# Fetching part of an embedding lookup row by row from a second DMA queue

## The chip, the cores and the metric

The kernel runs on one core of a Trainium2 chip. The core has a matrix engine (TensorE, PE in the profile), a vector engine (VectorE, DVE), a scalar engine (ScalarE, ACT), a general-purpose engine (GpSimd, POOL) and a synchronisation engine (SyncE, SP). Each engine works through its own instruction list in order and waits on semaphores for the others. Transfers between main memory and the on-chip memory are issued here by GpSimd (gathers, whose row addresses come from an index tile on the chip) and by SyncE (all other transfers). The metric is the time of one execution in device microseconds, lower is better. Before the change it is 5194.64 us, the median of 3 runs (5194.57 to 5196.89).

## The reference

A recommender model scores 16384 examples. Each has 32 token indices into a table of 50000 rows of 300 floats, 3 x 20 indices into small tables of 1000, 5000 and 10000 rows of 64, and 4 single indices into still smaller tables. The token rows and the multi-hot rows are averaged, everything is joined into 748 features, and a wide term adds one scalar per small-table index:

```python
tok = word_emb[token_idx].mean(axis=1)          # 32 rows of 300 each
e1 = emb_mh1[mh1_idx].mean(axis=1)              # e2, e3 alike, 20 rows of 64 each
o1 = emb_oh1[oh1_idx]                           # o2, o3, o4 alike
emb = jnp.concatenate([tok, e1, e2, e3, o1, o2, o3, o4], axis=1)
h = jax.nn.relu(emb @ W1 + b1)                  # 748 -> 1024
h = jax.nn.relu(h @ W2 + b2)                    # -> 512
h = jax.nn.relu(h @ W3 + b3)                    # -> 256
return jax.nn.sigmoid(h @ Wd + bd + wide)
```

## The kernel before

The batch is cut into 128 tiles of 128 examples. Three streams of work run beside each other for different tiles.

**Small tables by counting.** The small tables lie on the chip as `terms` (138 slices of 128 rows, each value split into three bf16 parts). For each example VectorE compares its indices with a ramp (`one_hots`, L344), ScalarE scales one half (L351), TensorE multiplies the two one-hot halves into a count per table row (`counts`, L362), and ScalarE writes the counts out (L365). A tile takes `STEPS` = 11 steps of six examples on each of two halves. In the 11 steps after that, TensorE multiplies the counts with `terms` (`small_sums`, L397, 138 products a tile in four groups that share one PSUM buffer `pg`), and VectorE evicts each group into the feature tile `g` (L387).

**Token rows by gathering.** `tokens()` issues, for each tile, 32 gathers on GpSimd (L279). One gather brings one token column, 128 rows of 1200 bytes, straight from the table. Two gathers fill one buffer of the pool `tok`; VectorE adds them into `tok_sum`, three pairs later in the program (`TOK_LAG`, lines L260 to L267). After the 16th pair the sum goes to `g`.

**Layers.** When a tile has its sums and its token sum, TensorE transposes `g` (L435) into the block `x`, VectorE scales it on the way out (L439). Three tiles form a block (the last two tiles are blocks of one). `mlp` runs the four layers of a block: `layer` (L493) with ScalarE's activations (L504), the last product `po` (L524), the final addition on VectorE (L529), the sigmoid (L530) and the store (L532).

The order is written out by hand in one loop over `n_steps` = 128 x 11 + `WAKE` steps. Everything that a step emits goes into each engine's list in that order. `toks.to(...)` spreads the gathers evenly over all steps; `layers.to(...)` spreads a block's layers from the step in which it becomes ready to the step in which the next one should be (`ready`, L586). `WAKE` = 16 steps come after the last counts, so the counts run ahead of the tokens by up to 16 steps. At `n_steps - EARLY` the first three feature chunks of the last tile are multiplied ahead (`early_part`, L457). If a block becomes ready while another is under way, the other one's remaining layers are emitted at once (L646). SyncE's list holds the index loads (L295, L300), the tables, the weights and the output stores.

Of the kernel before, what the change touches and what calls it, by code (L numbers as in the profile page):

```python
# [8 lines left out]
F32 = mybir.dt.float32  # L9
BF16 = mybir.dt.bfloat16  # L10
FP8 = mybir.dt.float8e3
I32 = mybir.dt.int32
# [6 lines left out]
P = 128  # L19
# [3 lines left out]
D1, D2, D3 = 1024, 512, 256  # L23
TOK_GROUP = 2
TOK_LAG = 3
TOK_BUFS = 7
HOT_BUFS = 3
WAKE = 16
EARLY = 3
BLOCK = 256  # L30
LAYER_TILES = 3
LAST_TILES = 2
# [30 lines left out]
def kernel(  # L63
# [33 lines left out]

    tokp = ctx.enter_context(tc.tile_pool(name="tok", bufs=TOK_BUFS))
    const = ctx.enter_context(tc.tile_pool(name="const", bufs=1))
    idxp = ctx.enter_context(tc.tile_pool(name="idx", bufs=3))  # L100
    keyp = ctx.enter_context(tc.tile_pool(name="keys", bufs=1))
    scp = ctx.enter_context(tc.tile_pool(name="sc", bufs=2))
    ohp = ctx.enter_context(tc.tile_pool(name="onehot", bufs=HOT_BUFS))
    cp = ctx.enter_context(tc.tile_pool(name="counts", bufs=2))
    gp = ctx.enter_context(tc.tile_pool(name="g", bufs=2))
    wp = ctx.enter_context(tc.tile_pool(name="wide", bufs=2))
    xp = ctx.enter_context(tc.tile_pool(name="x", bufs=2))
    hp = ctx.enter_context(tc.tile_pool(name="h", bufs=1))
# [56 lines left out]
    minus_count = const.tile([P, P], BF16, name="minus_count")  # L165
    nc.vector.tensor_single_scalar(minus_count, ident, -1.0 / COUNT, op=ALU.mult)

    def load_tables(part0, tag):
        raw = hp.tile([P, PART, ROW], F32, name="raw", tag=tag)
        for f in SMALL:  # L170
            table, (h0, h1) = tables[f], slices[f]
            full, rest = divmod(table.shape[0], P)
            a, b = max(h0, part0), min(h0 + full, part0 + PART)
            if a < b:
                nc.sync.dma_start(
                    out=raw[:, a - part0 : b - part0, :],
                    in_=table[(a - h0) * P : (b - h0) * P, :].rearrange("(h p) d -> p h d", p=P),
                )
            if rest and part0 <= h0 + full < part0 + PART:
                nc.vector.memset(raw[:, h0 + full - part0, :], 0.0)  # L180
                nc.sync.dma_start(out=raw[0:rest, h0 + full - part0, :], in_=table[full * P :, :])
        return raw

# [71 lines left out]

    def add_up(t, q, rows):

        a, b = rows[:, 0:TOK_D], rows[:, TOK_D : 2 * TOK_D]
        if q == 0:
            nc.vector.tensor_add(tok_sum, a, b)  # L260
        else:
            nc.vector.tensor_add(tok_sum, tok_sum, a)  # L262
            to = tok_sum
            if q == n_groups - 1:
                to = features(t)[:, TOK_AT:G_COLS]
                summed.add(t)
            nc.vector.tensor_add(to, tok_sum, b)  # L267

    def tokens():

        under_way = []
        for n in range(n_all):
            if n < n_all - TOK_LAG:
                t, q = divmod(n, n_groups)
                it = token_indices[t // NSUB][:, t % NSUB, :].bitcast(U32)
                rows = tokp.tile([P, TOK_GROUP * TOK_D], F32, name="tok_rows")
                for r in range(TOK_GROUP):
                    j = q * TOK_GROUP + r
                    nc.gpsimd.indirect_dma_start(  # L279
                        out=rows[:, r * TOK_D : (r + 1) * TOK_D],  # L280
                        out_offset=None,
                        in_=word,
                        in_offset=bass.IndirectOffsetOnAxis(ap=it[:, j : j + 1], axis=0),
                    )
                under_way.append((t, q, rows))
            if n >= TOK_LAG:
                add_up(*under_way.pop(0))
            yield 1

    def load_indices(blk):  # L290

# [121 lines left out]
    class Block:  # L413
# [2 lines left out]

        def __init__(self, first, n):
            self.first, self.n, self.missing = first, n * P, NK * n
            self.x = xp.tile([P, NK, N], F32, name="x")

        def transpose(self, t, ks):

# [34 lines left out]
    def early_part(block):  # L457


        part = []  # L460
        for pair in range(2):
            two = ps_c.tile([P, 2, 512], F32, name="pc")
            for m in range(2):
                part.append(two[:, m, :])
                for k in range(N_EARLY):
                    nc.tensor.matmul(
                        part[-1][:, 0 : block.n],
                        w1_sb[: chunk_k[k], k, (2 * pair + m) * P : (2 * pair + m + 1) * P],
                        block.chunk(k),
                        start=(k == 0),  # L470
                        stop=False,
                    )
        return part

    pending = []

    def flush_outputs():
        while pending:
# [2 lines left out]
    def layer(dst, weights, bias, srcs, n_out, part=None):  # L481


        n = srcs[0].shape[-1]
        for m in range(n_out):
            begun = part is not None and m < 4
            ph = part[m] if begun else ps_h.tile([P, N], F32, name="ph", tag="ph")
            for k, src in enumerate(srcs):
                if begun and k < N_EARLY:
                    continue  # L490
                if k == len(srcs) - 1:
                    flush_outputs()
                nc.tensor.matmul(  # L493
                    ph[:, 0:n],
                    weights[: src.shape[0], k, m * P : (m + 1) * P],
                    src,
                    start=(k == 0),
                    stop=(k == len(srcs) - 1),
                )
                if k < len(srcs) - 1:  # L500
                    yield 1

            def evict(m=m, ph=ph):
                nc.scalar.activation(dst[:, m, 0:n], ph[:, 0:n], AF.Relu, bias=bias[:, m : m + 1])  # L504

            pending.append(evict)
            yield 1

    def mlp(block, part=None):


        n = block.n
        h1 = hp.tile([P, M1, N], F32, name="h1", tag="odd")
        yield from layer(h1, w1_sb, b1_sb, [block.chunk(k) for k in range(NK)], M1, part)
        h2 = hp.tile([P, M2, N], F32, name="h2", tag="even")
        yield from layer(h2, w2_sb, b2_sb, [h1[:, k, 0:n] for k in range(M1)], M2)
        flush_outputs()
        h3 = hp.tile([P, M3 + 1, N], F32, name="h3", tag="odd")
        yield from layer(h3, w3_sb, b3_sb, [h2[:, k, 0:n] for k in range(M2)], M3)
        po = ps_h.tile([1, N], F32, name="po", tag="ph")  # L520
        for k in range(M3):
            if k == M3 - 1:
                flush_outputs()
            nc.tensor.matmul(  # L524
                po[:, 0:n], wd_sb[:, k : k + 1], h3[:, k, 0:n], start=(k == 0), stop=(k == M3 - 1)
            )
            yield 1
        y = h3[0:1, M3, 0:n]
        nc.vector.tensor_add(y, po[:, 0:n], block.wide())  # L529
        nc.scalar.activation(y, y, AF.Sigmoid, bias=bd_sb)  # L530
        b0 = block.first * P
        nc.sync.dma_start(out=out[b0 : b0 + n, :].rearrange("n o -> o n"), in_=y)  # L532

    class Paced:

# [50 lines left out]
    def ready(t):  # L586

        return max(-(-(n_groups * (t + 1) + TOK_LAG) * n_steps // n_all) + 1, (t + 2) * STEPS + 2)

    def block_for(t):  # L590
        if t not in block_of:
            n = ends[t] - t
            block = Block(t, n)
            block_of.update({t + k: block for k in range(n)})
        return block_of[t]
# [7 lines left out]
    sc, evict = key_columns(lookup_keys(ix))  # L603
    evict()
    hot = one_hots(sc, 0, 0)
    layers, cnt, sums, waiting = None, None, None, []
    for step in range(n_steps):
        t, i = divmod(step, STEPS)
        s = t % NSUB
# [24 lines left out]
            flush_outputs()  # L634
        if sums:
            run_sums(sums, early_sums.get(i, 0), step, step)
        if waiting and step >= waiting[0][0]:
            _, k, ks = waiting[0]
            if k in summed or ks[0] < N_EARLY and k == tiles - 1:
# [1 line left out]
                block = block_for(k)  # L641
                later.append((step, block.transpose(k, ks)))
                if not block.missing:
                    flush(step)
                    if layers:
                        layers.finish()  # L646
                    layers = Paced(mlp(block), LAYER_TIME * block.n / P)
                    last = block.first + block.n // P
                    begin, left = step, min(ready(ends[last] - 1) if last < tiles else n_steps, n_steps - EARLY) - step
        toks.to(n_all * (step + 1) / n_steps)  # L650
        if t < tiles and more and s == 1 and i == 5:
            next_sc, evict = key_columns(next_keys)
# [2 lines left out]
        if sums:  # L655
            ahead = n_h * (i + 1) / STEPS - sums_done[i + 1]
        if layers:
            layers.to(mlp_work * layers.size * (step + 1 - begin) / left + ahead)
        if sums:
            run_sums(sums, late_sums.get(i, 0), step, step + 1)  # L660
        flush(step)
        if i == 0 and 2 <= t <= tiles + 1:
            wide_term(features(t - 2))
            if t - 2 < tiles - 1:
# [3 lines left out]
                waiting.append((step + 2, t - 2, range(N_EARLY, NK)))  # L668
        if step == n_steps - EARLY:
            part = early_part(block_of[tiles - 1])  # L670
    layers.finish()
    for _, k, ks in waiting:
        block = block_for(k)
        block.transpose(k, ks)()
    Paced(mlp(block, part)).finish()
# [39 lines left out]
```

## Time and profile before

| | |
|---|---|
| median of 3 runs | 5194.64 us |
| the profiled execution | 5194.91 us, span 5193.1 us |
| TensorE busy | 4795.8 us (92%) |
| VectorE busy | 3733.3 us (72%) |
| ScalarE busy | 2720.9 us (52%) |
| GpSimd busy | 3877.1 us (75%), 4096 gathers of 0.946 us mean |
| transfers | 651.83 MB, 126 GB/s mean; the gathers occupy 44.7% of the 16 DMA engines' span |
| SyncE's queue | 16.53 MB, 1.4% |

A line of the groups reads: program line, engine, operation, tile written <- tiles read, count, then busy time and mean duration in ns, then the idle time of the engine just before these instructions and what ended most of it. "issue" is idle time in which the engine waited for nothing that the profile shows. A row of the stage table gives, after the stretch and its length, the busy time and the number of instructions of PE, PEld (weight loads), DVE, ACT and POOL, then the granted TensorE clock, the busy share of the DMA engines and GB/s. A line of the waits gives who waited, for whom, the total in us, how often, and the longest. Busy times of matrix products are modelled from pipelined records. SPq is SyncE's queue: the time is that of issuing a transfer, not of the transfer.

### The profile page before, as it was taken

How to read it: one execution, taken by the hardware profiler on the slowest of the kernel's cores; microseconds unless marked ns; L12 is line 12 of the kernel's file. 1: busy time of each engine (PE TensorE's matmuls, PEld its weight loads, DVE VectorE, ACT ScalarE, POOL GpSimd, SP SyncE). 2: the span in 40 equal slices, each digit the busy share in tenths (PEclk: the TensorE clock that was granted, in tenths of full speed). 3: DMA queues.
4: the chain of work that ended last, by engine and by line, in shares of the span. 5: the costliest groups of instructions: out<-in, count | busy, mean ns of one | idle time of the engine just before them, and what ended most of it. 6: DMA issues, size and time to landing. Idle time of an engine off the chain costs nothing.

```text
span 5193.1 us, 92066 instructions
## 1 busy us (share of the span) xinstructions
PE 4795.8 (92%) x34812; PEld 3528.0 (68%) x34812; DVE 3733.3 (72%) x6662; ACT 2720.9 (52%) x3538; POOL 3877.1 (75%) x4103
## 2 busy tenths in 40 slices
PE   7899999999999999999999999999999999999999
PEld 4666666666666766666676666666666766766677
DVE  6777777777777777777777777777777777777773
ACT  6555555555555555555555555555555555555552
POOL 6777777777777777777777777777777777777774
PEclk9899999999999999999999999999999999999999
DMA  7444444444444444444444444444444444444442
GB/s 193 125 126 125 125 126 125 125 126 125 125 126 125 126 125 125 125 125 125 126 125 126 125 125 126 125 125 126 125 126 126 124 126 125 125 125 124 126 124 71
DMA packets 253394, 651.83 MB, mean 126 GB/s; under 512 B 119547, under 2 KB 120103, under 8 KB 252947
## 3 DMA queue, kind: packets, MB, share of 16 engines
q0 software_dynamic: 196608, 629.41, 44.7%
q1 hardware_dynamic: 56339, 16.53, 1.4%
q8 instruction: 272, 4.46, 0.4%
q14 instruction: 175, 1.43, 0.1%
HBM read 645.59 MB, written 0.07 MB: 124 GB/s over the span
## 4 chain that ended last, share of the span: by engine, by line
PE 52%; DMA 16%; DVE 14%; issue 10%; POOL 6%; ACT 1%; DVEq 0%; POOLq 0%; ACTq 0%
PE ph L493 29%; PE pg L397 16%; DMA tok_rows<-in_word_emb_dram,it 16%; POOL tok_rows L279 6%; PE pc L362 5%; DVE hot L344 5%; DVE own L267 3%; DVE own L262 2%; DVE g L387 2%; PE po L524 1%; PE pc L435 1%; DVE x L439 1%; PE left L211 0%; ACT hot L351 0%; ACT cnt L365 0%
## 5 line engine op out<-in xcount | busy, mean ns | idle before, releaser
L279 POOL DMA_INDIRECT tok_rows<-in_word_emb_dram,it x4096 | 3876.2, 946 | 1283.3 <-issue 774.0
L351 ACT ACTIVATE hot<-hot 64x768 bf16<-64x768 bf16 (+1 forms) x1408 | 1155.4, 821 | 1630.4 <-DVE hot L344 1619.8
L397 PE MATMUL pg<-terms,cnt 128*128 128x195 bf16 x17664 | 1736.8, 248 | 291.9 <-DVE g L387 291.9
L397 PEld LDWEIGHTS <-cnt 128*128 128x128 fp8e3 x17664 | 1521.4, 98 | 50.5 <-issue 32.9
L493 PE MATMUL ph<-x,w_sb 128*128 128x384 f32 (+3 forms) x4176 | 1491.3, 490 | 56.7 <-DVE x L439 56.7
L344 DVE TENSOR_TENSOR hot<-own,sc 128x1656 bf16<-128x1656 bf16 (+1 forms) x1408 | 1393.7, 990 | 83.3 <-PE pc L362 2.1
L365 ACT ACTIVATE cnt<-pc 128x828 uint16<-128x828 f32 (+1 forms) x1408 | 1185.6, 842 | 501.3 <-PE pc L362 480.4
L493 PE MATMUL ph<-h,w_sb 128*128 128x384 f32 (+1 forms) x3520 | 1230.3, 486 | 0.5 <-ACT h L504 0.5
L267 DVE TENSOR_TENSOR own<-own,tok_rows 128x300 f32<-128x300 f32 x1792 | 857.1, 478 | 425.9 <-DMA tok_rows<-in_word_emb_dram,it 380.8
L493 PEld LDWEIGHTS ph<-x,w_sb 128*128 128x128 f32 (+1 forms) x4176 | 729.0, 192 | 579.1 <-issue 191.3
L262 DVE TENSOR_TENSOR own<-own,tok_rows 128x300 f32<-128x300 f32 x1920 | 917.4, 478 | 248.7 <-DMA tok_rows<-in_word_emb_dram,it 191.6
L362 PEld LDWEIGHTS <-hot 128*128 128x128 bf16 x8192 | 596.6, 98 | 517.4 <-issue 296.8
L493 PEld LDWEIGHTS ph<-h,w_sb 128*128 128x128 f32 x3520 | 618.8, 192 | 442.6 <-issue 150.8
L362 PE MATMUL pc<-hot 128*128 128x138 bf16 x8192 | 733.4, 225 | 28.5 <-ACT hot L351 25.7
L504 ACT ACTIVATE h<-ph,b_sb 128x384 f32<-128x384 f32 (+1 forms) x612 | 350.1, 572 | 255.4 <-PE ph L493 240.8
L387 DVE TENSOR_REDUCE g<-pg 128x130 f32<-128x390 f32 (+1 forms) x512 | 260.9, 510 | 295.2 <-PE pg L397 293.2
L439 DVE TENSOR_TENSOR x<-pc,scale 128x768 f32<-128x768 f32 x127 | 120.5, 949 | 70.9 <-PE pc L435 70.9
L260 DVE TENSOR_TENSOR own<-tok_rows 128x300 f32<-128x300 f32 x128 | 61.3, 479 | 83.3 <-DMA tok_rows<-in_word_emb_dram,it 81.0
L331 DVE COPY sc<-pc 128x512 bf16<-128x512 bf16 x64 | 44.1, 690 | 99.2 <-PE pc L327 99.2
L435 PE MATMUL pc<-ident,g 128*128 128x128 f32 x762 | 104.9, 274 | 0.4 <-ACT cnt L365 0.4
L529 DVE TENSOR_TENSOR h<-po,x 1x384 f32<-1x384 f32 (+1 forms) x44 | 23.4, 533 | 88.3 <-PE po L524 88.3
L267 DVE TENSOR_TENSOR g<-own,tok_rows 128x300 f32<-128x300 f32 x128 | 60.2, 470 | 35.6 <-DMA tok_rows<-in_word_emb_dram,it 32.6
(48 smaller groups left out, 456.6 us busy)
## 6 DMA issues: line engine op xcount, KB each, us to landing
tok_rows<-in_word_emb_dram,it POOLq DMA_INDIRECT x4096
ix<-in_idx_dram SPq DMA_DIRECT2D x128, 32.0 KB
w_sb<-in_W_dram SPq DMA_DIRECT2D x6, 512.0 KB
raw<-in_mh_dram SPq DMA_DIRECT2D x4, 682.5 KB
it<-in_idx_dram SPq DMA_DIRECT2D x64, 32.0 KB
w_sb<-in_W_dram SPq DMA_DIRECT2D x1, 2048.0 KB
out_dram<-h SPq DMA_DIRECT2D x42, 1.5 KB
raw<-in_mh_dram SPq DMA_DIRECT2D x2, 227.5 KB
```

The source lines that it names most:

```text
L262: nc.vector.tensor_add(tok_sum, tok_sum, a)
L267: nc.vector.tensor_add(to, tok_sum, b)
L279: nc.gpsimd.indirect_dma_start(out=rows[:, r * TOK_D : (r + 1) * TOK_D], out_offset=None, in_=word, in_offset=bass.IndirectOffsetOnAxis(ap ...
L344: nc.vector.tensor_tensor(hot[:, 0 : 2 * rows, :].rearrange("p i (n d) -> p i n d", d=2), iota.rearrange("p (n d) -> p n d", d=2).unsqueez ...
L351: nc.scalar.activation(upper, upper, AF.Copy, scale=UPPER)
L362: nc.tensor.matmul(pc[:, k // n, at : at + n_h], hot[:, 2 * k, 0:P], hot[:, 2 * k + 1, :], start=True, stop=True)
L365: nc.scalar.activation(cnt[:, :, b : b + rows].rearrange("l h (g k) -> l h g k", g=2), pc[:, :, 0 : n * n_h].rearrange("l g (k h) -> l h g ...
L387: nc.vector.tensor_reduce(field_columns(features(t), pair), pg[:, 0:n, :].rearrange("p f (c d) -> p f d c", c=3), AX.X, ALU.add,)
L397: nc.tensor.matmul(pg[:, j, :], by_slice[:, h, :], terms[:, h, :], start=(h == h0), stop=(h == h1 - 1))
L439: nc.vector.tensor_tensor(self.x[:, ks[0] : ks[-1] + 1, at : at + P].rearrange("p (a c) b -> p a c b", a=banks), pt, scale[:, ks[0] : ks[- ...
L493: nc.tensor.matmul(ph[:, 0:n], weights[: src.shape[0], k, m * P : (m + 1) * P], src, start=(k == 0), stop=(k == len(srcs) - 1),)
L504: nc.scalar.activation(dst[:, m, 0:n], ph[:, 0:n], AF.Relu, bias=bias[:, m : m + 1])
```

## The change

In two of every three tiles from tile 2 on (84 tiles), the last of the 32 token columns is no longer gathered by GpSimd. Instead SyncE loads the 128 indices of that column into one partition (`column`), reads them 16 at a time into its registers, and issues one transfer per row, 128 transfers of 1200 bytes, into a tile `fetched`. VectorE adds that tile as the last addend of the tile's token sum. The issues are emitted in a window of `FETCH_STEPS` = 17 steps that begins `FETCH_AHEAD` = 21 steps before the sum is due; windows of neighbouring tiles overlap, and then the issues of both are interleaved. A few other things change with it:

- `WAKE` is 27 in place of 16, so there are 1435 steps in place of 1424.
- Buffers: `tok` 6 (was 7), `onehot` 2 (was 3), `idx` 4 (was 3), `g` 3 (was 2), two `fetched`.
- A block that becomes ready goes into a list `complete`. Near the end it waits there until the block under way is through; the last three-tile block is to be done `LAST_LAYERS` = 6 steps before the end.
- The last addition, the sigmoid and the store of a block (`finish`) are emitted one step later than before.
- `early_part` begins six of the eight outputs of layer 1 for the last tile in place of four, the other two in the `pg` bank. The last block's `x` lies in a `counts` buffer.
- The padding rows of the raw tables are zeroed by a transfer from a tile of zeros in place of a VectorE memset.

```diff
-TOK_BUFS = 7
-HOT_BUFS = 3
-WAKE = 16
+TOK_BUFS = 6
+HOT_BUFS = 2
+FETCH_FROM = 2
+FETCH_STEPS = 17
+FETCH_AHEAD = 21
+LOADS = 16
+WAKE = 27
 EARLY = 3
+LAST_LAYERS = 6
...
-                nc.vector.memset(raw[:, h0 + full - part0, :], 0.0)
+                nc.sync.dma_start(out=raw[rest:P, h0 + full - part0, :], in_=zeros[rest:P, :])
...
-                rows = tokp.tile([P, TOK_GROUP * TOK_D], F32, name="tok_rows")
+                tok_rows = tokp.tile([P, TOK_GROUP * TOK_D], F32, name="tok_rows")
+                rows = []
                 for r in range(TOK_GROUP):
                     j = q * TOK_GROUP + r
+                    if j == N_TOK - 1 and t in fetched:
+                        rows.append(fetched.pop(t))
+                        continue
+                    rows.append(tok_rows[:, r * TOK_D : (r + 1) * TOK_D])
                     nc.gpsimd.indirect_dma_start(
...
+    def fetch(t):
+        rows = fp.tile([P, TOK_D], F32, name="fetched")
+        column = fp.tile([1, P], I32, name="column")
+        nc.sync.dma_start(
+            out=column, in_=idx[t * P : (t + 1) * P, N_TOK - 1 : N_TOK].rearrange("n o -> o n")
+        )
+        for p0 in range(0, P, LOADS):
+            _, values = nc.values_load_multi_w_load_instructions(
+                column[:, p0 : p0 + LOADS],
+                engines=[mybir.EngineType.SP],
...
+            )
+            for i, value in enumerate(values):
+                p = p0 + i
+                nc.sync.dma_start(out=rows[p : p + 1, :], in_=word[bass.ds(value, 1), :])
+                if p == P - 1:
+                    fetched[t] = rows
+                yield 1
...
-        y = h3[0:1, M3, 0:n]
-        nc.vector.tensor_add(y, po[:, 0:n], block.wide())
...
+        def finish():
+            y = h3[0:1, M3, 0:n]
+            nc.vector.tensor_add(y, po[:, 0:n], block.wide())
...
+        rows_out.append(finish)
...
+    fetches = []
+    for t in range(FETCH_FROM, tiles):
+        if t % 3 != 1:
+            fetches.append((int(summed_at(t)) - FETCH_AHEAD, Paced(fetch(t))))
+
+    def deadline(block):
+        last = block.first + block.n // P
+        ahead = tiles - 1 - last
+        if ahead == 1 and block.n > P:
+            return n_steps - LAST_LAYERS
+        return ready(ends[last] - 1) if ahead > 0 else n_steps
...
                 if not block.missing:
-                    flush(step)
-                    if layers:
-                        layers.finish()
-                    layers = Paced(mlp(block), LAYER_TIME * block.n / P)
...
+                    complete.append(block)
+        if complete and (layers is None or layers.done >= layers.total or complete[0].first + complete[0].n // P < tiles - 1):
+            flush(step)
+            block = complete.pop(0)
+            if layers:
+                layers.finish()
+            layers = Paced(mlp(block), LAYER_TIME * block.n / P)
...
+        while fetches and step >= fetches[0][0] + FETCH_STEPS:
+            fetches.pop(0)[1].finish()
+        for at, rows in fetches[:2]:
+            rows.to(P * (step + 1 - at) / FETCH_STEPS)
```

More of the change, by code (lines that the diff above doesn't have):

```diff
@@ L99 @@
     const = ctx.enter_context(tc.tile_pool(name="const", bufs=1))
-    idxp = ctx.enter_context(tc.tile_pool(name="idx", bufs=3))
+    idxp = ctx.enter_context(tc.tile_pool(name="idx", bufs=4))
     keyp = ctx.enter_context(tc.tile_pool(name="keys", bufs=1))
@@ L104 @@
     cp = ctx.enter_context(tc.tile_pool(name="counts", bufs=2))
-    gp = ctx.enter_context(tc.tile_pool(name="g", bufs=2))
+    fp = ctx.enter_context(tc.tile_pool(name="fetched", bufs=2))
+    gp = ctx.enter_context(tc.tile_pool(name="g", bufs=3))
     wp = ctx.enter_context(tc.tile_pool(name="wide", bufs=2))
@@ L166 @@
     nc.vector.tensor_single_scalar(minus_count, ident, -1.0 / COUNT, op=ALU.mult)
+    zeros = const.tile([P, ROW], F32, name="zeros")
+    nc.vector.memset(zeros, 0.0)
     def load_tables(part0, tag):
@@ L256, in add_up @@
     def add_up(t, q, rows):
-        a, b = rows[:, 0:TOK_D], rows[:, TOK_D : 2 * TOK_D]
+        a, b = rows
         if q == 0:
@@ L275, in tokens @@
                 it = token_indices[t // NSUB][:, t % NSUB, :].bitcast(U32)
-                rows = tokp.tile([P, TOK_GROUP * TOK_D], F32, name="tok_rows")
+                tok_rows = tokp.tile([P, TOK_GROUP * TOK_D], F32, name="tok_rows")
+                rows = []
                 for r in range(TOK_GROUP):
                     j = q * TOK_GROUP + r
+                    if j == N_TOK - 1 and t in fetched:
+                        rows.append(fetched.pop(t))
+                        continue
+                    rows.append(tok_rows[:, r * TOK_D : (r + 1) * TOK_D])
                     nc.gpsimd.indirect_dma_start(
-                        out=rows[:, r * TOK_D : (r + 1) * TOK_D],
+                        out=rows[-1],
                         out_offset=None,
@@ L288, in tokens @@
             yield 1
+    fetched = {}
+    def fetch(t):
[8 more added lines that the diff above has]
+                engines=[mybir.EngineType.SP],
+                min_val=0,
+                max_val=word.shape[0] - 1,
+                skip_runtime_bounds_check_because="the indices are rows of the table",
+            )
[5 more added lines that the diff above has]
+                yield 1
     def load_indices(blk):
@@ L418, in __init__ @@
             self.first, self.n, self.missing = first, n * P, NK * n
-            self.x = xp.tile([P, NK, N], F32, name="x")
+            if first + n < B // P:
+                self.x = xp.tile([P, NK, N], F32, name="x")
+            else:
+                self.x = cp.tile([P, NK, n * P], F32, name="x_last", tag="counts")
         def transpose(self, t, ks):
@@ L462, in early_part, with flush_rows @@
             two = ps_c.tile([P, 2, 512], F32, name="pc")
[L463 to L472, printed above, removed]
-        return part
-    pending = []
+            part += [two[:, 0, :], two[:, 1, :]]
+        part.append(ps_g.tile([P, 2, 3 * ROW], F32, name="pg").rearrange("p f d -> p (f d)"))
+        for m, to in enumerate(part):
+            for k in range(N_EARLY):
+                nc.tensor.matmul(
+                    to[:, 0 : block.n],
+                    w1_sb[: chunk_k[k], k, m * P : (m + 1) * P],
+                    block.chunk(k),
+                    start=(k == 0),
+                    stop=False,
+                )
+        return part
+    pending, rows_out = [], []
+    def flush_rows():
+        while rows_out:
+            rows_out.pop(0)()
     def flush_outputs():
@@ L485, in layer @@
         for m in range(n_out):
-            begun = part is not None and m < 4
+            begun = part is not None and m < len(part)
             ph = part[m] if begun else ps_h.tile([P, N], F32, name="ph", tag="ph")
@@ L512, in mlp @@
         n = block.n
+        flush_rows()
         h1 = hp.tile([P, M1, N], F32, name="h1", tag="odd")
@@ L527, in mlp @@
             yield 1
-        y = h3[0:1, M3, 0:n]
-        nc.vector.tensor_add(y, po[:, 0:n], block.wide())
-        nc.scalar.activation(y, y, AF.Sigmoid, bias=bd_sb)
-        b0 = block.first * P
-        nc.sync.dma_start(out=out[b0 : b0 + n, :].rearrange("n o -> o n"), in_=y)
+        def finish():
+            y = h3[0:1, M3, 0:n]
+            nc.vector.tensor_add(y, po[:, 0:n], block.wide())
+            nc.scalar.activation(y, y, AF.Sigmoid, bias=bd_sb)
+            b0 = block.first * P
+            nc.sync.dma_start(out=out[b0 : b0 + n, :].rearrange("n o -> o n"), in_=y)
+        rows_out.append(finish)
     class Paced:
@@ L588, in ready, with summed_at @@
         return max(-(-(n_groups * (t + 1) + TOK_LAG) * n_steps // n_all) + 1, (t + 2) * STEPS + 2)
+    def summed_at(t):
+        return (n_groups * (t + 1) + TOK_LAG) * n_steps / n_all
+    fetches = []
[8 more added lines that the diff above has]
+        return ready(ends[last] - 1) if ahead > 0 else n_steps
     def block_for(t):
@@ L605 @@
     hot = one_hots(sc, 0, 0)
-    layers, cnt, sums, waiting = None, None, None, []
+    layers, cnt, sums, waiting, complete = None, None, None, [], []
     for step in range(n_steps):
@@ L636 @@
             run_sums(sums, early_sums.get(i, 0), step, step)
+        outputs = list(rows_out)
         if waiting and step >= waiting[0][0]:
@@ L643 @@
                 if not block.missing:
-                    flush(step)
-                    if layers:
-                        layers.finish()
-                    layers = Paced(mlp(block), LAYER_TIME * block.n / P)
-                    last = block.first + block.n // P
-                    begin, left = step, min(ready(ends[last] - 1) if last < tiles else n_steps, n_steps - EARLY) - step
+                    complete.append(block)
[5 more added lines that the diff above has]
+            layers = Paced(mlp(block), LAYER_TIME * block.n / P)
+            layers.total = mlp_work * layers.size
+            begin, left = step, max(deadline(block) - step, 1)
+        while fetches and step >= fetches[0][0] + FETCH_STEPS:
+            fetches.pop(0)[1].finish()
+        for at, rows in fetches[:2]:
+            rows.to(P * (step + 1 - at) / FETCH_STEPS)
         toks.to(n_all * (step + 1) / n_steps)
@@ L657 @@
         if layers:
-            layers.to(mlp_work * layers.size * (step + 1 - begin) / left + ahead)
+            layers.to(mlp_work * layers.size * min((step + 1 - begin) / left, 1) + ahead)
+            if layers.done >= layers.total:
+                layers.finish()
         if sums:
@@ L661 @@
         flush(step)
+        if outputs and rows_out[: len(outputs)] == outputs:
+            flush_rows()
         if i == 0 and 2 <= t <= tiles + 1:
@@ L670 @@
             part = early_part(block_of[tiles - 1])
-    layers.finish()
+    while complete or layers:
+        layers.finish()
+        layers = Paced(mlp(complete.pop(0))) if complete else None
     for _, k, ks in waiting:
@@ L675 @@
     Paced(mlp(block, part)).finish()
+    flush_rows()
 def kernel(**inputs):
```

## The prediction

> **What bounds the kernel now.** I read the page first (busy time by engine, then the groups), then the stage table for the steady part and the end, then the waits, last the SyncE records.
>
> ```profile
> PE 4795.8 (92%) x34812; PEld 3528.0 (68%) x34812; DVE 3733.3 (72%) x6662; ACT 2720.9 (52%) x3538; POOL 3877.1 (75%) x4103
> L279 POOL DMA_INDIRECT tok_rows<-in_word_emb_dram,it x4096 | 3876.2, 946 | 1283.3 <-issue 774.0
> ```
>
> ```profile
> 1000.00:2000.00 1000.00, 931.61 (x6768) 683.47 (x6767) 729.98 (x1299) 528.15 (x681) 756.44 (x800) 0.99 0.46 125
> 5100.00:5193.00 93.00, 86.39 (x604) 70.04 (x603) 23.44 (x51) 15.76 (x38) 26.54 (x29) 1.00 0.18 50
> ```
>
> The busy shares name TensorE (92%), but GpSimd is the pace-maker. Its 75% hides that each gather is 0.946 us busy and then about 0.30 us idle with nothing to wait for: in the steady stretch 800 gathers fill 1000 us exactly, 1.25 us each. 4096 x 1.25 = 5120 of the 5193.1 us. Only the end differs: 29 gathers in the last 93 us.
>
> ```profile
> POOL tok_rows L279 <- issue: 774.0, 2541, 0.3
> PE pg L397 <- DVE g L387: 159.9, 150, 2.8
> PE ph L493 <- DVE x L439: 43.2, 23, 2.3
> DVE own L267 <- DMA tok_rows<-in_word_emb_dram,it: 225.7, 362, 2.5
> ```
>
> (The first line is of the whole span, the other three of 1000 to 4000 us.) GpSimd's gaps have no releaser. VectorE waits for token rows. TensorE waits about twice a tile for the eviction of the shared `pg` bank and once a block for the last transposes; most single waits in the trace sit at 0.65 and 1.77 us, the time of an eviction and its hand-over, which a faster token stream does not remove. So there are two near-bounds: GpSimd at 100%, TensorE at 93% plus these fixed waits.
>
> ```profile
> 85.16 0.29 SPq L242 DMA_DIRECT2D bd_sb<-in_bd_dram  x1
> L532 SPq DMA_DIRECT2D out_dram<-h x44: 227/268/283, 294.4 to 5190.8; - x44
> L295 SPq DMA_DIRECT2D it<-in_idx_dram x64: 373/374/4843, 0.7 to 4897.1; - x64
> 0.75 1.98 DMA it<-in_idx_dram
> ```
>
> These four say what SyncE pays: 0.27 to 0.29 us to issue a transfer of one row, 0.37 us for one of 256 rows of 128 bytes, and 1.98 us from issue to landing.
>
> **The change part by part, against the profiled span of 5193.1 us** (the launch itself read 5194.91, the median of three is 5194.64, so 1.8 us lie outside and the profiled run stands 0.3 us over the median).
>
> *84 gathers removed from GpSimd.* 84 x 1.25 = -105.0 us on the pace-maker. The gain is whole only while SyncE delivers and TensorE keeps up.
>
> *10752 single-row transfers on SyncE.* The instruction order of the changed kernel shows, for each of 84 tiles: one transfer of the 128 indices, 8 register loads of 16 indices, 128 register operations and 128 one-row transfers. One row: 0.268 (the output row) + 0.045 gap between SyncE records + a register operation that I set equal to a semaphore record with its gap, 0.028 + 0.031: 0.372 us. Ends: 0.31 if the register operation costs nothing, 0.48 if an address from a register makes it as dear as the 0.374 issue. I take 0.372, because the output row has the same shape, one row of about 1.5 KB. The index column must land before the first load: 0.6 issue (like the 128-line `b_sb` loads, 0.61 us) + 2.0 landing = 2.6 us. The index loads and the output store, which share this queue, are 1.5 us per fetched tile. So a fetched tile costs SyncE 128 x 0.372 + 2.6 + 1.5 = 51.7 us plus 8 register loads L. Two such tiles come in three tile times; a token tile is then 16 / 1.429 = 11.19 steps of 3.495 us = 39.1 us, so 58.7 us are there for each. SyncE holds if L is under 0.87 us. No row shows a register load from on-chip memory: the low end is a semaphore record, 0.028 us, the high end a whole transfer, 1.98 us. It reads 64 bytes without a transfer, so it is nearer the low end; I take 0.5 us, 55.7 us a tile, hidden under the 58.7. What waits behind SyncE's own waits: once in three tiles the output store waits for ScalarE's sigmoid, and all rows behind it too. SyncE then starts level with the program, and the rows are programmed to end 4 steps (14 us) before the sum; two tiles take 111 us against 28.2 steps x 3.5 + 14 = 113. VectorE waits for late rows, then the token buffers fill and GpSimd stops. At the start SyncE reaches the first fetch only after the table loads (about 64 us) and the weights push in (15 us): tiles 2 and 3 come up to 10 us late, most of it inside the six buffered pairs. Term: +5, ends -10 (a VectorE stall of 10.4 us on the replaced memset goes) and +25.
>
> The Trainium skill, "Runtime: NRT & Kernel Launch", section "Instruction fetch mechanics", speaks against this: about 200 ns per register even in bulk. By that 16 registers take an estimated 3.2 us, a fetched tile 77 us, and the kernel some 6600 us. "DMA: Bandwidth & Descriptors", section "Latency and other measured facts", gives a register load a floor near 600 ns, which would fit. No row here decides between them.
>
> *TensorE, next in line.* The new pace is 4012 gathers in 1435 steps: 2.796 x 1.25 = 3.495 us a step, 38.4 us for the 11 steps of a count tile. TensorE before: 11 steps x 2.876 gathers x 1.25 = 39.54 us a tile, of which 0.9316, 36.84 us, busy; the layers (1491 + 1230 us of L493) spread over 1435 steps in place of 1424 give -0.16; fixed waits 2 x 0.654 + 0.54 (23 of 1.77 us in the 76 tiles of the stretch) = 1.85. Sum 38.5. So it needs as much as GpSimd, and the excess of today's waits (2.70 idle a tile against 1.85) decides. Ends: 0 if the excess goes, 128 x (39.38 - 38.44) = +120 if it all stays. The excess comes from evictions queued behind VectorE's token waits, which shrink, so I take a quarter of it: +25.
>
> *Counts 27 steps ahead and the queue of last blocks.* Before, GpSimd stopped twice near the end (9.3 and 19.2 us between gathers in place of 1.25) because VectorE was held behind TensorE's backlog: 26 us. Eleven more steps without counts relieve that; but the work that TensorE then has (the last three-tile block of about 59 us, sums 12, two single tiles of 21 each) fills the 94 us of 27 steps and the 33 us from the last gather's start. Term -10, ends -26 and +10.
>
> *Edits taken as nothing.* Six token buffers: in the trace a gather starts at least 2.4 us after the addition that frees the buffer six pairs earlier (from the 60th pair to near the end), so GpSimd would not wait. Two one-hot buffers: VectorE now writes 233 of 1408 before TensorE is done with the tile two steps earlier (190 us in all). Its covers are VectorE's idle 27% and the 3.9 us median by which one-hots are ready before TensorE needs them; without them up to 190 us. Late output (`finish` a step later) removes VectorE's 88.3 us waits for `po`, all hidden. Two more early partial sums: 6 matmuls of 0.275 us, under 2 us. Zeros by transfer: seven small issues before 65 us.
>
> Sum: 5193.1 - 105.0 + 5 + 25 - 10 = 5108.1, plus 1.8 outside: **5110 us**, 1.6% less.
>
> **The rivals.**
>
> *SyncE becomes the bound (ends slower).* Place: the SyncE queue. It paces the kernel when a fetched tile costs more than 58.7 us; total = 79 (start) + 84 x cost + 30 (tail). Break-even with before at 60.5 us a tile: L = 1.1 us, or L = 0.5 with rows at 0.44. At L = 1.5 it gives 79 + 84 x 63.7 + 30 = 5460 us; at L = 1.98, 5780. For it: SyncE would run at 95% even by my prices, and every price is of other transfers. Against it: a load without a transfer should not cost most of one.
>
> *TensorE keeps its waits.* All 2.70 us a tile stay: 5193.1 - 105 + 5 + 120 - 10 + 1.8 = 5205 us, no change. For it: 92% busy. Against: median waits already sit at the floor.
>
> *The rows come, but all on few DMA engines, and gathers land late.* The output row shows just one landing of data, so a row uses one engine. A 1.5 KB packet is 0.066 us; 10752 of them are 0.7 ms on one engine that is 46% busy: no bound, about 5110 still.
>
> **How the numbers follow.** The main case has 60%, its own range 5054 (all low ends: -105 - 10 - 26) to 5165 (+80 of TensorE's 120). TensorE's rival 8%, 5165 to 5205; SyncE's 30%, 5150 to 5800, of which a tenth still ends faster; 2% for the rest. A measurement of this kernel tells 0.2% (10 us) from no change: faster 0.66, same 0.04, slower 0.30. The range goes from 5050 to 5460: below lie 4%, above about half of SyncE's case.
>
> **What would show it.** Right: GpSimd 4012 gathers still at 1.25 us without releasers, TensorE busy 94 to 95%, SyncE rows at 0.35 to 0.40 us spacing, VectorE waits for `fetched` near zero, no long gaps near the end. Wrong: VectorE waiting long for `fetched`, GpSimd with long waits for VectorE each third tile, SyncE solid from start to end (first rival); GpSimd waiting for buffers while TensorE waits for `pg` at over 1 us (second).

## The result and the profile after

The changed kernel takes 5923.54 us (median of 5 runs, 5919.22 to 5925.04), 1.1401 times the time before, with a 95% interval of 1.1387 to 1.1415. The forecast of 5110 us was wrong in sign; the rival "SyncE becomes the bound" happened, and beyond the upper end of the range.

The chain of work that ended last, by engine, in the page of the kernel before:

```profile
PE 52%; DMA 16%; DVE 14%; issue 10%; POOL 6%; ACT 1%; DVEq 0%; POOLq 0%; ACTq 0%
```

The same line in the page of the changed kernel, and the groups in which the new waits stand:

```profile
SPq 44%; PE 29%; issue 17%; DVE 5%; DMA 4%; ACT 1%; POOL 1%; DVEq 0%; ACTq 0%; POOLq 0%
...
L293 POOL DMA_INDIRECT tok_rows<-in_word_emb_dram,it x4012 | 3795.4, 946 | 2082.8 <-issue 883.6
...
L276 DVE TENSOR_TENSOR g<-own,fetched 128x300 f32<-128x300 f32 x84 | 39.5, 470 | 706.6 <-DMA fetched<-in_word_emb_dram 684.1
```

SyncE's queue, which before appeared nowhere in the chain, is its largest part. A gather still takes 0.946 us, but GpSimd's idle time rose from 1283 to 2083 us. VectorE stood 684 us before the 84 additions that take the fetched rows.

The stage table of the changed kernel, the stretch that was shown of before (after the stretch and its length: busy time and instructions of PE, PEld, DVE, ACT, POOL, then the clock, the DMA share and GB/s):

```profile
1000.00:2000.00 1000.00, 842.93 (x5939) 616.31 (x5940) 644.14 (x1139) 465.96 (x599) 646.15 (x683) 0.93 0.41 110
```

683 gathers in 1000 us in place of 800, TensorE 84% busy in place of 93%, VectorE 64% in place of 73%. For whom the engines wait, the waits say:

```profile
DVE g L276 <- DMA fetched<-in_word_emb_dram: 684.1, 56, 40.1
POOL tok_rows L293 <- DVE own L276: 480.2, 348, 14.3
POOL tok_rows L293 <- DVE own L269: 457.4, 62, 36.1
ACT h L551 <- DMA out_dram<-h: 373.7, 39, 15.6
```

The first line starts the sequence that the prediction describes: rows late, VectorE stopped, token buffers full, GpSimd stopped. (The fourth line comes up again in the experiments.)

SyncE's own records, first by line and tile (count, then shortest, median and longest duration in ns, first and last start), then a stretch of its queue in order of time:

```profile
L324 SPq DMA_DIRECT2D fetched<-in_word_emb_dram x10752: 224/225/299, 73.8 to 5837.4; - x200
L324 SPq MOVE fetched<-in_word_emb_dram x10752: 29/29/39, 73.7 to 5837.4; - x200
L324 SPq FUSED_REGOPS  x10752: 37/37/51, 73.6 to 5837.3; - x200
L315 SPq TENSOR_LOAD <-column x672: 1131/1230/1437, 72.4 to 5829.8; - x168
```

```profile
2006.18 0.56 SPq L311 DMA_DIRECT2D column<-in_idx_dram  x1
2010.36 48.82 SPq L324 DMA_DIRECT2D fetched<-in_word_emb_dram  x98
2059.28 0.56 SPq L311 DMA_DIRECT2D column<-in_idx_dram  x1
2063.00 35.92 SPq L324 DMA_DIRECT2D fetched<-in_word_emb_dram  x78
```

The rows run from 73.8 to 5837.4 us. Between the first of them and the last no gap in the queue is over 5 us. So the time up to there is SyncE's: 84 tiles from 70.0 to 5837.4 us are 68.7 us each. This divides the span of 5922.9 us, it does not test anything; the experiments do that. The remaining 85.5 us are TensorE's. The chain that ended last, in order of time (start, duration in us, what), shows the change of hands:

```profile
5815.68 0.23 SPq L324
5816.01 1.11 DMA out_dram<-h
5817.22 0.59 ACT h L551
5831.31 25.84 PE ph L540 x80
5899.65 0.49 PE pt L477 x3
```

(Lines between these are left out.) An output store stood behind rows in SyncE's queue, and ScalarE waited 15.6 us for its landing; then TensorE works almost without a pause through the layers of the last three-tile block and the last two tiles. Tile 127, which is gathered after the last fetched tile, has its token sum at 5882 us, but TensorE takes it up only at 5899.65 us.

Summing durations and gaps of SyncE's records from 70.0 to 5837.4 us, and dividing by 84, gives what a fetched tile costs:

| part | predicted, us | measured, us |
|---|---|---|
| 128 rows | 47.6 (0.372 each) | 53.76 (0.420 each) |
| 8 register loads of 16 | 4.0 (0.5 each) | 10.15 (1.27 each, gap included) |
| column: issue and wait | 2.6 | 2.60 |
| index loads, stores, weights | 1.5 | 2.16 |
| sum | 55.7 | 68.66 |

A row is three records: a register operation (`FUSED_REGOPS`) 0.037 us, a register move (`MOVE`) 0.029, the transfer 0.225 median (0.227 mean), and 0.126 of gaps between them. The move is not in the instruction order that the prediction read; every one of the 10752 transfers with an address from a register has one, and none of the 10752 with a fixed address has (below).

### The profile page after: what moved, and what is told of

It is laid out like the page before. It is cut to its first block, busy times and chain, and to the rows that moved or that the text cites. A ratio compares the mean times of both kernels' runs of the same rounds, so it can differ in the third digit from the quotient of the medians.

```text
span 5922.9 us, 125380 instructions
## 1 busy us (share of the span) xinstructions
PE 4946.9 (84%) x34812; PEld 3610.1 (61%) x34812; DVE 3748.9 (63%) x6656; ACT 2720.5 (46%) x3538; POOL 3796.3 (64%) x4019
## 4 chain that ended last, share of the span: by engine, by line
SPq 44%; PE 29%; issue 17%; DVE 5%; DMA 4%; ACT 1%; POOL 1%; DVEq 0%; ACTq 0%; POOLq 0%
SPq L324 34%; PE ph L540 15%; PE pg L436 10%; SPq L315 9%; PE pc L401 3%; DVE hot L383 2%; DMA column<-in_idx_dram 1%; DVE own L271 1%; POOL tok_rows L293 1%; DVE g L426 1%; DMA out_dram<-h 1%; DVE own L276 1%; SPq L339 1%; DMA tok_rows<-in_word_emb_dram,it 1%; ACT hot L390 1%
## 5 line engine op out<-in xcount | busy, mean ns | idle before, releaser
L293 POOL DMA_INDIRECT tok_rows<-in_word_emb_dram,it x4012 | 3795.4, 946 | 2082.8 <-issue 883.6
L436 PE MATMUL pg<-terms,cnt 128*128 128x195 bf16 x17664 | 1788.2, 253 | 375.3 <-DVE g L426 373.0
L436 PEld LDWEIGHTS <-cnt 128*128 128x128 fp8e3 x17664 | 1562.2, 100 | 98.3 <-issue 71.7
L540 PE MATMUL ph<-x,w_sb 128*128 128x384 f32 (+2 forms) x4128 | 1514.4, 500 | 77.6 <-ACT h L551 60.5
L540 PE MATMUL ph<-h,w_sb 128*128 128x384 f32 (+1 forms) x3520 | 1261.6, 495 | 0.0
L401 PE MATMUL pc<-hot 128*128 128x138 bf16 x8192 | 749.4, 228 | 276.7 <-ACT hot L390 260.8
L276 DVE TENSOR_TENSOR g<-own,fetched 128x300 f32<-128x300 f32 x84 | 39.5, 470 | 706.6 <-DMA fetched<-in_word_emb_dram 684.1
L477 PE MATMUL pc<-ident,g 128*128 128x128 f32 x762 | 117.7, 290 | 185.2 <-DVE g L276 175.7
L477 PEld LDWEIGHTS pc<-ident,g 128*128 128x128 f32 x762 | 88.7, 150 | 225.8 <-DVE g L276 180.0
L572 PE MATMUL po<-h,wd_sb 128*1 128x384 f32 (+1 forms) x176 | 82.8, 568 | 44.6 <-ACT h L551 44.3
```

Source lines behind the costliest of these rows:

```text
L293: nc.gpsimd.indirect_dma_start(out=rows[-1], out_offset=None, in_=word, in_offset=bass.IndirectOffsetOnAxis(ap=it[:, j : j + 1], axis=0),)
L401: nc.tensor.matmul(pc[:, k // n, at : at + n_h], hot[:, 2 * k, 0:P], hot[:, 2 * k + 1, :], start=True, stop=True)
L436: nc.tensor.matmul(pg[:, j, :], by_slice[:, h, :], terms[:, h, :], start=(h == h0), stop=(h == h1 - 1))
L540: nc.tensor.matmul(ph[:, 0:n], weights[: src.shape[0], k, m * P : (m + 1) * P], src, start=(k == 0), stop=(k == len(srcs) - 1),)
```

## The experiments

Theory S: SyncE's queue alone is the bound, the rest of the change behaves as predicted. Rival T: the rest of the schedule (smaller pools, 27 steps ahead, queue of blocks) costs the time. Rival D: the one-row transfers, by traffic or late landing, disturb the gathers.

**No tile fetched.**

```diff
-        if t % 3 != 1:
+        if False:
```

> No tile is fetched by SyncE, all 4096 gathers are back on GpSimd; everything else of the change stays (27 steps ahead, smaller pools, queue of blocks). Theory S (SyncE's queue is the bound, nothing else of the change costs much): 5165 to 5195 us, since 4096 gathers at 1.25 us are 5120 us and only the end can get shorter. Rival T (the rest of the schedule, two one-hot buffers above all, costs the time): 5400 us or more.

Measured: 5178.04 us, ratio 0.9967 (0.9955 to 0.998). Theory T falls: the rest of the change gains 17 us.

**One tile in three.**

```diff
-        if t % 3 != 1:
+        if t % 3 == 2:
```

> 42 tiles fetched in place of 84, nothing else changed. Theory S: a fetched tile costs SyncE 68 us of the 117 us that three tiles take, so the queue has slack and 42 gathers less give 52 us: 5115 to 5150 us. Rival D (the one-row transfers disturb the gathers on the DMA engines): half of the loss stays, about 5500 us. Rival T: 5400 us or more.

Measured: 5152.55 us, ratio 0.9917 (0.9901 to 0.9934). Half the rows of the changed kernel, and the loss is gone; D's 5500 us did not come. The time is 2.5 us over the range of S, and the 42 gathers less won only 25 us against the run without fetching, where 50 were due. The waits of VectorE in this kernel, from 0 to 300 us, show two single long ones:

```profile
DVE g L276 <- DMA fetched<-in_word_emb_dram: 17.8, 1, 17.8
DVE low L351 <- DMA ix<-in_idx_dram: 17.3, 2, 15.3
```

The rows of the first fetched tile, and the indices that stand behind rows in the queue, come late once, at the start. Over the whole span VectorE has no other wait for fetched rows.

**84 last tokens left out.** In place of the fetched tile a tile of zeros is added.

```diff
-                    if j == N_TOK - 1 and t in fetched:
-                        rows.append(fetched.pop(t))
+                    if j == N_TOK - 1 and t >= FETCH_FROM and t % 3 != 1:
+                        rows.append(zeros)
```

> Leaves out the last token of 84 tiles: neither gathered nor fetched, a tile of zeros is added in its place. SyncE has no rows to send. This prices the rest of the prediction's sum, 84 gathers less with TensorE next in line: the prediction's terms without SyncE's give 5105 us. If TensorE keeps all its waits: 5200 us.

Measured: 5078.57 us, ratio 0.9776 (0.976 to 0.9792). Against the kernel with no tile fetched, 84 gathers less are 99.5 us, 1.18 us each of the 1.25 they could bring. TensorE's waits of this kernel from 1000 to 4000 us:

```profile
PE pg L436 <- DVE g L426: 145.3, 156, 2.5
PE ph L540 <- DVE x L481: 8.4, 8, 1.1
```

Before these were 159.9 and 43.2 us; TensorE follows a faster token stream almost all the way.

**Rows from fixed numbers.** The transfers stay, the register work goes.

```diff
-            _, values = nc.values_load_multi_w_load_instructions(
...
+            values = [997 * t % 49000 + 131 * (p0 + i) for i in range(LOADS)]
...
-                nc.sync.dma_start(out=rows[p : p + 1, :], in_=word[bass.ds(value, 1), :])
+                nc.sync.dma_start(out=rows[p : p + 1, :], in_=word[value % 50000 : value % 50000 + 1, :])
```

> All 10752 one-row transfers stay in the same two tiles of three, but from row numbers fixed in the program: no register loads, no register operations, no wait for the column of indices (the output is of other rows). Theory S: a fetched tile costs SyncE about 128 x 0.32 + 2 = 43 us, under the 58.7 us available: 5090 to 5140 us. Rival D (the traffic or the landings of the one-row transfers): 5700 us or more.

Measured: 5086.58 us (one run), 3 us under S's range. All 10752 transfers cost some 8 us beside none at all, so D falls, and 837 us of the changed kernel hang on how the addresses get into the transfers: the register loads, the register operations and moves, and the wait for the column. Its transfers and VectorE's additions, then what SyncE's queue waits for:

```profile
L318 SPq DMA_DIRECT2D fetched<-in_word_emb_dram x10752: 219/246/443, 70.0 to 4984.3; - x200
L276 DVE TENSOR_TENSOR g<-own,fetched x84: 469/470/472, 151.1 to 5003.6; 128x300 f32<-128x300 f32 x84
its engine sat idle before it (us, times) until:
  DMA fetched<-in_word_emb_dram: 16.0, 1
```

```profile
SPq L576 <- ACT h L574: 1564.7, 44, 53.0
```

The transfer itself is no shorter; VectorE waits for rows once, 16 us, in place of 684 us, and SyncE now has time to wait 1565 us for the results that it is to store.

**Register loads of 8.**

```diff
-LOADS = 16
+LOADS = 8
```

> The changed kernel with register loads of 8 indices in place of 16, 1344 loads. Says what a register load's 1.23 us consists of. If the price is per load: 672 more loads of 1.28 us, 860 us more, about 6780 us. If it is per register (0.077 us each): loads of 0.62 us, only gaps are added, about 5960 us. Either way theory S wants the kernel's time to move one to one with SyncE's.

Measured: 6196.27 us (one run), between the two prices, and the record says why:

```profile
L315 SPq TENSOR_LOAD <-column x1344: 682/782/975, 71.7 to 6105.9; - x192
```

0.782 us for 8 registers and 1.230 for 16: 0.056 us per register and 0.33 per load. SyncE's loads with their gaps, without the waits for the column, grew by 256 us (852.6 to 1108.2), the kernel by 273 (one run): nearly one to one, as S wants.

**Every second tile, later start.**

```diff
-FETCH_FROM = 2
-FETCH_STEPS = 17
-FETCH_AHEAD = 21
+FETCH_FROM = 6
+FETCH_STEPS = 20
+FETCH_AHEAD = 24
...
-        if t % 3 != 1:
+        if t % 2 == 0:
```

> Every second tile fetched, but only from tile 6 on (61 tiles), window of 20 steps that begins 24 ahead. Theory S: SyncE pays 68 us of the 78 us of two tiles. The kernel with one tile in three lost 25 us that its 42 gathers should have won; its trace shows a wait of 15 us for indices and one of 18 us for the first fetched tile, both at the start. If the start is the cause: 5178 - 61 x 1.19 = 5105 us, up to 5120. If late rows in the steady part were the cause: 5140 us or more.

Measured: 5109.82 us, ratio 0.9827 (0.9811 to 0.9844); VectorE waits for no fetched tile. The code of the changed kernel, with a smaller share and a later start, is faster than before by the gathers that it saves, so the start explains what one tile in three lacked. (Start, window and lead were changed together; which of them does it is not separated.)

**Byte addresses.** Two tiles of three again, from tile 5. Columns of 32 tiles are loaded at once and multiplied by 1200 on VectorE, four instructions of 0.2 us median, so the register needs no operation.

```diff
+    def load_columns(k):
+        columns[k] = const.tile([GROUP, P], I32, name=f"columns{k}")
...
+        nc.vector.tensor_single_scalar(columns[k], columns[k], 4 * TOK_D, op=ALU.mult)
...
-                nc.sync.dma_start(out=rows[p : p + 1, :], in_=word[bass.ds(value, 1), :])
+                nc.sync.dma_start(out=rows[p : p + 1, :].bitcast(mybir.dt.uint8), in_=word_bytes[0:1, bass.ds(value, 4 * TOK_D)])
```

> Two tiles of three from tile 5 on (82 tiles), still from indices in registers, but the columns are loaded for 32 tiles at a time and multiplied by 1200 on VectorE once, so that the register holds the byte address: no register operation per row, no transfer and no wait for a column per tile. Theory S: 128 x 0.33 + 8 x 1.28 + 1.5 = 54 us a tile, under the 58.6 available: 5080 to 5115 us. If SyncE's queue were not what costs the time: 5700 us.

Measured: 5085.87 us, ratio 0.9782 (0.9766 to 0.9799), the best version here that computes everything. A row is 0.334 us, a fetched tile about 55 us, 94% of the 58.6 us available, and VectorE waits for no fetched tile. The share of tiles is the changed kernel's but for the first two; what was taken away is 13 us of SyncE's time per tile.

**Five tiles of seven.**

```diff
-        if t % 3 != 1:
+        if t % 7 not in (1, 4):
```

> The same with five tiles of seven (88 tiles): SyncE's 54 us stand against 54.7 us. Theory S puts this at the edge: 5075 to 5100 us if the queue just holds, 5100 to 5200 us if the store that waits in the same queue takes the last slack.

Measured: 5276.35 us, ratio 1.0147 (1.013 to 1.0164). Six fetched tiles more than the last kernel, 190 us lost: worse than either expectation. The work alone, about 55 us a tile against 54.7, is too long by an estimated 26 us over 88 tiles. SyncE's queue waited 283.0 us before stores, VectorE 295.3 us for rows.

**The stores issued by ScalarE**, once in the five-of-seven kernel, once in the changed one.

```diff
-            nc.sync.dma_start(out=out[b0 : b0 + n, :].rearrange("n o -> o n"), in_=y)
+            nc.scalar.dma_start(out=out[b0 : b0 + n, :].rearrange("n o -> o n"), in_=y)
```

> The kernel with five tiles of seven, but the output stores are issued by ScalarE in place of SyncE, 44 issues. Its SyncE needs about 55 us a fetched tile, 4850 us in all, and yet rows were late by 295 us while the queue itself waited 283 us for ScalarE ahead of stores. If that wait inside the queue is the cause: SyncE runs ahead and the time falls to 5070 to 5110 us. If the 55 us against 54.7 us are the cause alone: 5200 us or more.

> The changed kernel with only that edit. Its profile shows ScalarE waiting 374 us for the landing of stores that stand behind rows in SyncE's queue. Theory S: SyncE's queue has next to no gaps, so this is no second cause: 5890 to 5925 us. If ScalarE's wait were on the path: 5550 to 5700 us.

Measured: 5545.42 us (ratio 1.0679, 1.0661 to 1.0697) and 6004.12 us (one run), the second outside both of its expectations. Both got slower, so this does not isolate the wait. A wait of SyncE's queue in the first of them:

```profile
SPq L335 <- DMA out_dram<-h: 495.8, 40, 36.4
```

The transfers of both queues share eight completion semaphores in turn in this program. A row whose turn is a store's semaphore waits until that store has landed, wherever it was issued, so the wait for ScalarE came back under another name. In the changed kernel ScalarE's wait for the store fell from 373.7 to 1.2 us without making it faster, while SyncE's queue got 132.6 us of new waits for stores. This gives no sign of a second cause, but it does not exclude a small one: at the end the wait for the store is on the chain (above), and there the time from the last row to the end fell from 85.5 to 77.3 us.

**More lead for the rows.** Five tiles of seven, the stores on SyncE, rows begun 32 steps ahead, three fetched tiles under way at once, the scaled columns in two buffers in place of four. On two other chips this kernel took 7451 and 7463 us, but there the kernel before, too, took 7529 and 7526 us; why is not known, and they are not used.

```diff
-FETCH_AHEAD = 21
+FETCH_AHEAD = 32
...
-    fp = ctx.enter_context(tc.tile_pool(name="fetched", bufs=2))
+    fp = ctx.enter_context(tc.tile_pool(name="fetched", bufs=3))
...
-        for at, rows in fetches[:2]:
+        for at, rows in fetches[:3]:
```

> The same kernel a third time, since in both runs before the kernel before itself took about 7530 us. Expected as there: 5070 to 5110 us if the lead of the rows was what five tiles of seven lacked; 5200 us or more if SyncE's work is simply too much.

Measured: 5191.21 us, ratio 0.9996 (0.9986 to 1.0005), between both expectations. VectorE waits for no fetched tile now, but ScalarE waits for stores:

```profile
ACT h L563 <- DMA out_dram<-h: 155.4, 12, 26.9
```

A store stands behind more rows in the queue, and the first layer of the next block may not overwrite the buffer that the store reads (`h3` and `h1` share it). So with SyncE this full, either the rows wait behind the store or the store behind the rows. That the lead moves the wait from one to the other is shown by these two runs (VectorE for rows 295.3 to 0 us, ScalarE for stores 48.6 to 155.4 us); how much of the 190 us each is worth is not separated.

## Why the prediction was wrong

- **The step that failed is SyncE's term, "SyncE holds if L is under 0.87 us", with L taken as 0.5 us.** The register load measured 1.23 us, 1.27 with its gap. Its two bounds (0.028 and 1.98 us) held and lay far apart, and the choice between them, "nearer the low end" because no transfer is involved, was an argument without a row. So SyncE's work was not hidden under GpSimd's: at 68.7 us a tile against 58.7 it became the bound, as the first rival describes.
- **The row's price was low too:** 0.420 against 0.372, inside the ends 0.31 to 0.48. The unseen register move with the gap before it (0.069 us) and a dearer register operation (0.089 with its gap, against 0.059) more than account for it; the transfer was cheaper than assumed (0.262 with its gap, against 0.313). Each miss alone costs about 6 us a tile and would have put the sum near 62 us, over the 58.7 available. The prediction put the break-even with L = 0.5 at rows of 0.44 us; its own sum, 128 rows + 2.6 + 1.5 + 4.0 = 60.5, gives 0.41, which the measured row alone exceeds.
- **The rival's formula held, its last term did not.** 79 + 84 x 68.7 + 30 gives 5880; measured 5922.9 span. The start was 9 us shorter, the tail 55 us longer: 85.5 us, because TensorE still has the layers of the last three-tile block, begun late, and of two single tiles to do.
- **The margin would have done, with the right prices.** The predicted prices put SyncE at 95% of its time. Byte addresses, at 94%, held and came within the forecast's range; 55 us of 54.7 (five tiles of seven), about 101%, lost 190 us; nothing between was measured. The prediction saw that the store waits in the same queue, but priced only the rows behind the store, not the store behind the rows.
- **The range** stopped at 5460, where half of the rival's own span lay above. The load was inside the rival's bounds, but rows and load together, 68.7 us a tile, went beyond its dearest case (L = 1.98: 67.5 us a tile, 5780 us), and the tail came on top.
- **Right:** GpSimd is the pace-maker, although "no releaser" fits only 774.0 of its 1283.3 us of gaps (most of the others the profile puts down to VectorE); a gather less is worth 1.18 of 1.25 us (99.5 us for 84). The schedule's part (term -10, measured -17), the two one-hot buffers (VectorE waits 160.7 us for TensorE in the kernel with rows left out, hidden), six token buffers, and the rival of few DMA engines (8 us) came out about as costed. The sum without SyncE's +5 was 5105; the run without rows took 5078.6, mostly because TensorE's +25 was about 5 (1.25 x 84 - 99.5). With SyncE's work cut to 55 us a tile (byte addresses), the forecast's mechanism works, at 5085.87 us.

The trace also settles what no row could before. The Trainium skill, "Runtime: NRT & Kernel Launch", section "Instruction fetch mechanics", gives some 200 ns per register, for registers loaded from main memory; by it 16 would take an estimated 3.2 us. This load from on-chip memory took 1.23 us, 0.056 for each register more. Taken for this load, as the prediction did, the page's figure had the right sign and over twice the size. The 600 ns floor of "DMA: Bandwidth & Descriptors", section "Latency and other measured facts", agrees: it lies below every load here, the shortest 0.682 us (8 registers).

## What to carry to other kernels

An engine that is idle in the profile is not free capacity until the price of every instruction that it will get is known, the address work included: count instructions per unit and compare with the time per unit before moving work there. If a price has no row and its bounds enclose the break-even, let the bounds set the chances; here either of two such prices alone, a load of 1.27 us in place of 0.5 or a row dearer by 0.05 us, puts a tile near 62 us, past the rival's break-even of 60.5. A queue that others wait for, and that itself waits for others, loses more than its excess of work (here 190 us with an estimated 26 us too much). And the same move pays (here 2.2%, of which the rest of the change gives 0.3%) once the per-row address work is done for many rows at a time on another engine.

## What was not expected of the hardware

- Loading 16 registers from on-chip memory holds SyncE 1.23 us, 8 registers 0.78 us.
- A one-row transfer with its address from a register is two records, a move of 0.029 us and an issue of 0.225 us; the changed kernel has a register operation of 0.037 us ahead of them. With fixed addresses the issue alone is 0.246 us median, but the row together costs 0.30 in place of 0.42 us (3228 us of durations and gaps for 10752 rows).
- In the changed kernel, where TensorE was busy 84% of the time in place of 92%, its granted clock was 0.928 (before 0.99), and its busy time rose from 4795.8 to 4946.9 us with the same number of products (34812). The clock was 0.99 again in every version in which SyncE keeps up. What lowers it is not shown.
